# Two recurrent layers of a four-layer kernel: the state copies on ScalarE, and the group norm's power in two halves

## The chip, the cores and the metric

The kernel runs on one core of a Trainium2 chip. The core has a matrix engine (TensorE, PE in the profile; its weight loads are PEld), a vector engine (VectorE, DVE), an engine for activations (ScalarE, ACT), a programmable engine (GpSimd, POOL) and an engine that here only issues transfers (SyncE, SP). Each engine works through its own queue in order, and they meet through semaphores. The metric is the device time of one execution in microseconds (us), given as the median of several runs.

## The reference

Four layers run one after another on x of shape (4, 512, 512): an attention layer with 32 query heads and 8 key heads, two recurrent layers, and a last attention layer with an MLP of four times the width. The change touches the two recurrent layers alone. What they compute, for one batch, is this:

```python
k, v, w, r, g = ...                      # products of five mixes of x with its shifted self
w = exp(-exp(w))                         # per step and channel, in 32 heads of 16
def step(s, inp):                        # s: 16 x 16 state per head
    a = k_l[..., :, None] * v_l[..., None, :]
    out = einsum('bhs,bhst->bht', r_l, faaaa * a + s)
    return a + w_l[..., None] * s, out
y = scan over 512 steps of step
y = (y - mean(y)) * rsqrt(var(y) + 1e-5) # over the 16 channels of a head
x = x + (y * gn_w + gn_b) * silu(g) @ Wo.T
x = x + sigmoid(xr @ fWr.T) * (square(relu(xk @ fWk.T)) @ fWv.T)
```

The state starts from rows of the context `ctx_2048`, and everything is float32.

## The kernel before

The function `recurrent` cuts the two layers into 16 units (q = 0 to 15): layer, batch, and one of two halves of 256 time steps. An even q is a first half; an odd q continues it from the state that the even one left. A unit is computed by three generators, `mixes` (layer norm, mixes and the products k, v, r, g, w), `outputs` (group norm and Wo) and `channels` (the second part of the layer). In between runs the recurrence itself, in G = 8 groups per unit, with a running number g = 8q + (0 to 7).

The recurrence takes two time steps at once. For a group, `begun` multiplies on VectorE the spread-out v (vr, in PSUM) by k into two tiles, kv for the second and A for the first step of each pair (line 833), copies the start state S into column 0 of kv (line 839, VectorE), and adds A to kv with an accumulating transfer that GpSimd issues (`added`, line 584). ScalarE spreads the decay into W (line 844). `scan` then runs the scan over kv (line 862, VectorE), in even units copies the last column back into S (line 864, VectorE), and multiplies by r into two tiles ry (line 867, VectorE). `summed` sums ry over the channels on TensorE (py, line 881), and `taken` adds py to y (line 894, VectorE). The tile A has one buffer, kv two, and vr one.

The order of the work is written out by hand. The loop over g runs from before 0 to 28 beyond the last group (g = 128 = `end`); in every turn it calls `summed(g - 1)`, `begun(g + 1)`, `scan(g)`, and every fourth time `repeated` (vr, line 814), and then the pieces that are due in this turn, in four phases EARLY, SOON, MID and LATE. A generator's `yield 11, EARLY` says that its next piece belongs to turn 8q + 11, phase EARLY; `follow` appends it to the list `steps[(turn, phase)]`. So `outputs(q)` starts at turn 9 of its unit, while the unit q + 1 is in its group 1, and `channels(q)` at turn 19. What is called first stands first in each engine's queue. From turn 129 on, one piece of layer 3 (`beside`) is called after each turn's pieces.

The group norm of `outputs` is spread over these turns: the mean (turn 9), y minus the mean (line 909), the squares on ScalarE (line 912), the variance on TensorE (line 917), variance plus 1e-5 into `rstd`, a tile gn_rs of 128 x 64 (line 927, VectorE, turn 10 LATE), the power -1/2 on GpSimd (line 929, turn 11 EARLY), four copies into rp on ScalarE (line 933, turn 12 LATE), a product that spreads it over the channels (pbc, line 935; bc on ScalarE, line 938), and y times it (line 940). Then follow yg on ScalarE (line 945) and its product with the gate on GpSimd (line 952), and Wo.

In GpSimd's queue, the power of unit q - 1 stands in turn 8q + 3. Behind it stand, as `channels` and `mixes` of other units fall due: the small power of the next layer norm (rs_cx, line 79) with ln_mv (line 552), in the layers' later units the two transfers x<-xr (line 584), then the kv<-A of the next turn, mix_g<-xa, and the kv<-A of the turn after it. ScalarE's queue in an even unit has, in its groups 0 to 7 and among much else: al (line 792), mix (line 665), td (line 735), o_w (lines 744 and 750, twice exponential), o_v (line 702), bc (line 938), yg (line 945), and xk and xr (line 990). The gate is o_g: ScalarE writes its tanh (line 698) after GpSimd's yg has left that tile, and VectorE's line 717 finishes it, which frees a PSUM tile for TensorE's transposes ptn (line 572).

Of the kernel before, what the change touches and what calls it, by code (L numbers as in the profile page):

```python
# [11 lines left out]
ALU = mybir.AluOpType  # L12
# [18 lines left out]
def tile_xattn_rwkv_perceiver(ctx: ExitStack, tc: tile.TileContext, t: dict, out: bass.AP):  # L31
    nc = tc.nc
# [7 lines left out]
    mhalf = const.tile([P, TS // 4], F32, name="mhalf")  # L40
# [30 lines left out]
    def mm(ps, pairs):  # L71
        for i, (lhsT, rhs) in enumerate(pairs):
            nc.tensor.matmul(ps, lhsT, rhs, start=(i == 0), stop=(i == len(pairs) - 1))  # L73
# [22 lines left out]
    def psum_tile(shape, name):  # L96
        pool, tag = psum["p"]
        return pool.tile(shape, F32, tag=tag, name=name)
# [356 lines left out]
    def recurrent(lp, ep, beside):  # L455
# [5 lines left out]
        TP = TS // 2  # L461
        EARLY, SOON, MID, LATE = range(4)
# [67 lines left out]
        def flat(a):  # L530
            return a.rearrange("p a l -> p (a l)")
# [314 lines left out]
        def place(g):  # L846
            q, j = divmod(g, G)
            return q, j // NI, j % NI

        def quarters(kv):  # L850
            return kv.rearrange("p (q f) l -> p q f l", f=2)

        def states(q):
            return st[q]["S"].rearrange("p i (q e f) -> p i e q f", e=2, f=2)

        def scan(g):

            q, e, i = place(g)
            d = st[q]
            kv = kvs.pop(g)  # L860

            nc.vector.tensor_tensor_scan(flat(kv), flat(W[g % 2]), flat(kv), 0.0, ALU.mult, ALU.add)  # L862
            if units[q][2] == 0:
                nc.vector.tensor_copy(states(q)[:, i, e], quarters(kv)[:, :, :, TP])
            for h in range(2):
                y = ys[g, h] = mp.tile([P, 4, 2, TP], F32, tag="ry", name="ry", bufs=4)
                nc.vector.tensor_tensor(  # L867
                    y,
                    kv[:, 4 * h : 4 * h + 4, None, :TP].to_broadcast([P, 4, 2, TP]),
                    d["r"][:, i].rearrange("p (o m) -> p o m", o=2)[:, None].to_broadcast([P, 4, 2, TP]),  # L870
                    ALU.mult,
                )
# [23 lines left out]
        def outputs(q):  # L896

            li, b, hf = units[q]
            n = f"L{li}_"
            c, d = small[li], st[q]  # L900
            y = d["y"]
            NQ = TS // 4
            full = [P, NI, TS]
            pm = psum_tile([P, TS], "pmean")
            mm(pm, [(gmean, y[:, i, :]) for i in range(NI)])
            mean = sq.tile([P, TS], F32, tag="mean", name="mean", bufs=1)
            nc.scalar.copy(mean, pm)
            yield 9, LATE
            nc.vector.tensor_tensor(y, y, mean[:, None, :].to_broadcast(full), ALU.subtract)
            yield 10, EARLY  # L910
            y2 = mq.tile(full, F32, tag="cx", name="y2", bufs=BUFS["cx"])
            nc.scalar.activation(y2, y, AF.Square)
            yield 10, SOON
            var = psum_tile([P, NQ], "var")
            for i in range(NI):
                for a in range(4):
                    nc.tensor.matmul(
                        var[32 * a : 32 * a + 32],
                        gm32,
                        y2[:, i, NQ * a : NQ * a + NQ],  # L920
                        start=(i == 0),
                        stop=(i == NI - 1),
                        tile_position=(0, 32 * a),
                    )
            yield 10, LATE
            rstd = sq.tile([P, NQ], F32, tag="gn_rs", name="gn_rs")
            nc.vector.tensor_scalar(rstd, var, 1.0, 1e-5, ALU.mult, ALU.add)  # L927
            yield 11, EARLY
            nc.gpsimd.tensor_tensor(rstd, rstd, mhalf[:, :NQ], ALU.pow)  # L929
            yield 12, LATE  # L930
            for a in range(4):
                rs = slice(32 * a, 32 * a + 32)
                nc.scalar.copy(rp[rs, NQ * a : NQ * a + NQ], rstd[rs])
            yield 13, EARLY
            pm = psum_tile([P, TS], "pbc")
            mm(pm, [(gself, rp)])
            bc = sq.tile([P, TS], F32, tag="mean", name="bc", bufs=1)
            nc.scalar.copy(bc, pm)
            yield 13, LATE
            nc.vector.tensor_tensor(y, y, bc[:, None, :].to_broadcast(full), ALU.mult)  # L940
            yield 14, EARLY

            yg = mq.tile(full, F32, tag="cx", name="yg", bufs=BUFS["cx"])
            for i in range(NI):
                nc.scalar.activation(
                    yg[:, i].rearrange("p (m o) -> p o m", o=2),
                    y[:, i].rearrange("p (o m) -> p o m", o=2),
                    AF.Identity,
                    bias=c["gn"][:, i, 1:2],
                    scale=c["gn"][:, i, 0:1],  # L950
                )
            nc.gpsimd.tensor_tensor(yg, yg, d["g"], ALU.mult)
            yield 15, MID
            wo = wpool.tile([P, NI, C], F32, tag="w", name=n + "wo")
            for a in range(4):
                nc.sync.dma_start(
                    wo[32 * a : 32 * a + 32], t[n + "Wo"].rearrange("(h a i) n -> a h i n", a=4, i=NI)[a]
                )
            pms = []
            for lt in range(NT):  # L960
                pm = psum_tile([P, C], "pm")
                mm(pm, [(yg[:, i, lt * P : (lt + 1) * P], wo[:, i, :]) for i in range(NI)])
                pms.append(pm)
            yield 15, LATE
            for lt in range(NT):
                x = xn[b][hf * NT + lt]
                nc.vector.tensor_tensor(x, pms[lt], x, ALU.add)
# [74 lines left out]
        steps = {}  # L1042
# [6 lines left out]
        for q in range(len(units)):  # L1049
            if q > 0:  # L1050
                follow(q, (-13 if q == 1 else -11, LATE), mixes(q))
            follow(q, (9, EARLY), outputs(q))
            follow(q, (19, LATE), channels(q))
# [3 lines left out]
        with ExitStack() as below, ExitStack() as above:  # L1057
# [14 lines left out]
            for g in range(at[0], end + 28):  # L1072
                if 0 < g <= end:
                    summed(g - 1)
                if -1 <= g < end - 1:
                    begun(g + 1)
                if 0 <= g < end:
                    scan(g)
                if 0 < g < end - 2 and g % NI == NI - 2:
                    repeated(*place(g + 2)[:2])  # L1080
                for ph in (EARLY, SOON, MID, LATE):
                    for q, gen in steps.pop((g, ph), ()):
                        at = next(gen, None)
                        if at:
                            follow(q, at, gen)
                    if ph == MID and 0 < g <= end and g % NI == 0:
                        taken(g - 1)
                if g == end:
                    above.close()
                elif g > end:  # L1090
                    next(beside, None)
# [336 lines left out]
    with tc.manual_schedule(engines={E.PE, E.DVE, E.Activation, E.Pool}), ExitStack() as both:  # L1428
        lp = both.enter_context(tc.tile_pool(name="rl", bufs=1))
        ep = both.enter_context(tc.tile_pool(name="rt", bufs=2))  # L1430
        third = layer3()
        ahead = recurrent(lp, ep, iter(third.__next__, "closed"))
        layer0(ahead, ep)
        for _ in ahead:
            pass
        both.close()
        for _ in third:
            pass
# [64 lines left out]
```

## Time and profile before

| What | us |
|---|---|
| median of 3 runs | 3747.28 (3745.63 to 3757.73) |
| the profiled execution | 3749.93 |
| its span | 3748.2 |
| granted clock of TensorE, mean | 0.971 |
| first scan to last scan (line 862) | 782.8 to 2282.2 |

The span runs from the first instruction to the last; 1.7 us of the execution lie around it. Layer 0 fills about the first 780 us, the recurrent layers run to about 2440 us, their last part beside the start of layer 3, which then runs alone to the end. A unit of the recurrent layers takes some 98 us.

A row of the profile names the line, the engine, the operation and the tiles written and read; "x16" is how often it ran, and after the bar stand its busy time in all, the mean of one in ns, and the idle time of its engine just before it with what ended that. In a timeline a row has the start, the length, the engine and the instruction, and in brackets the idle time before it with what ended it. These are the rows of the page that belong to the recurrence:

| row | count | mean ns |
|---|---|---|
| line 862, VectorE, scan | 128 | 2316 |
| line 867, VectorE, ry | 256 | 1416 |
| line 833, VectorE, A | 128 | 1217 |
| line 584, GpSimd, issue of kv<-A | 127 | 936 |
| line 881, TensorE, py | 1024 | 631 |

The copies of line 864 took 172 to 2302 ns, median 174, 64 of them.

### The profile page before, as it was taken

The page shows a single profiled execution, that of the slowest core. Times are in us where ns is not written, and L with a number is a line of the kernel's source. Part 1 is how long each engine was busy: PE and PEld are TensorE (multiplying, and loading weights), DVE is VectorE, ACT ScalarE, POOL GpSimd, SP SyncE. Part 2 cuts the span into 40 slices and gives each one's busy share as a digit, 9 for nine tenths or more (in the row PEclk, how much of TensorE's full clock was granted, in tenths as well). Part 3 has the DMA queues.
Part 4 walks back from the last instruction along what each step waited for, and adds up shares of the span by engine and source line. Part 5 has one row for each costly group of instructions (what it writes and reads, how often), then busy time and mean ns, then how long its engine had stood idle before and what let it go on. Part 6 is the DMA issues. An engine that isn't in the chain of part 4 may idle for free.

```text
span 3748.2 us, 52355 instructions
## 1 busy us (share of the span) xinstructions
PE 3561.1 (95%) x20544; PEld 1894.1 (51%) x20544; DVE 2748.8 (73%) x4665; ACT 1667.2 (44%) x2486; POOL 1762.1 (47%) x834
## 2 busy tenths in 40 slices
PE   9999999998899999999999996999999999999989
PEld 3333333365565656656556653544455444544446
DVE  6777777679988888888988884388856666667531
ACT  4776776533444444444444432233344334334421
POOL 4777777524444444444444444155533433444430
PEclk9999998999899999999999998999999999999999
DMA  4000000056577777777777775410022112121223
GB/s 153 24 12 23 12 9 20 24 142 136 136 174 177 167 178 180 171 167 175 177 169 176 168 183 125 118 35 15 26 82 79 60 56 96 60 71 35 96 96 123
DMA packets 188805, 386.66 MB, mean 103 GB/s; under 512 B 18128, under 2 KB 44880, under 8 KB 186512
## 3 DMA queue, kind: packets, MB, share of 16 engines
q1 hardware_dynamic: 150256, 251.72, 21.3%
q0 software_dynamic: 38304, 131.61, 19.0%
q8 instruction: 162, 2.65, 0.3%
q14 instruction: 83, 0.68, 0.1%
HBM read 247.50 MB, written 4.19 MB: 67 GB/s over the span
## 4 chain that ended last, share of the span: by engine, by line
PE 72%; DVE 12%; DMA 5%; issue 4%; POOL 3%; ACT 3%; SPq 0%; POOLq 0%; DVEq 0%; ACTq 0%
PE pm L73 10%; PE ph L73 6%; PE pv L73 6%; PE po L73 6%; DMA kv<-A 5%; PE psc L242 5%; PE pst L279 5%; PE pst L1186 4%; PE psc L1186 4%; PE po L1252 3%; PE po L304 3%; PE pr L73 3%; PE pk L73 3%; DVE ry L867 3%; DVE kv L862 2%
## 5 line engine op out<-in xcount | busy, mean ns | idle before, releaser
L1247 POOL TENSOR_TENSOR acc<-acc,aT 128x2048 f32<-128x2048 f32 x96 | 436.2, 4544 | 337.9 <-ACT aT L1242 219.9
L292 POOL TENSOR_TENSOR aT<-aT,nmT 128x1536 f32<-128x1536 f32 x124 | 428.6, 3460 | 207.6 <-ACT aT L290 184.3
L254 DVE CUSTOM_DVE_ANT_0 sc<-psc,nm 128x512 f32<-128x512 f32 x512 | 354.1, 692 | 147.0 <-PE psc L242 89.3
L1231 DVE TENSOR_TENSOR aT<-pst,mb 128x512 f32<-128x512 f32 x512 | 317.8, 683 | 162.7 <-PE pst L1186 162.7
L867 DVE TENSOR_TENSOR ry<-kv,o_r 128x1024 f32<-128x1024 f32 x256 | 352.0, 1416 | 3.5
L862 DVE TENSOR_TENSOR_SCAN kv<-W,kv 128x1032 f32<-128x1032 f32 x128 | 296.4, 2316 | 0.2 <-DMA kv<-A 0.2
L584 POOL DMA_DIRECT2D kv<-A x127 | 118.9, 936 | 367.6 <-DVE kv L839 364.5
L290 ACT COPY aT<-pst 128x512 f32<-128x512 f32 x372 | 196.6, 595 | 178.0 <-PE pst L279 177.5
L298 ACT ACTIVATE aT<-aT 128x2048 f32<-128x2048 f32 x128 | 246.7, 1929 | 5.3 <-POOL aT L292 4.6
L73 PE MATMUL ph<-nT,l_m 128*128 128x256 f32 x1024 | 238.1, 388 | 0.0
L73 PE MATMUL po<-l_m,hT 128*128 128x512 f32 x512 | 233.1, 601 | 0.0
L73 PEld LDWEIGHTS ph<-nT,l_m 128*128 128x128 f32 x1024 | 193.4, 193 | 64.4 <-issue 24.8
L1200 DVE CUSTOM_DVE_ANT_0 sc<-psc,zeros,mx 128x512 f32<-128x512 f32 x256 | 176.7, 747 | 57.8 <-PE psc L1186 48.7
L279 PE MATMUL pst<-q,km 32*128 32x512 f32 x1024 | 206.4, 641 | 9.5 <-DVE mxs L254 5.8
L833 DVE TENSOR_TENSOR A<-vr,o_k 128x1024 f32<-128x1024 f32 x128 | 155.8, 1217 | 73.5 <-DMA kv<-A 73.5
L1242 ACT ACTIVATE aT<-aT 128x2048 f32<-128x2048 f32 x64 | 122.3, 1911 | 191.6 <-DVE aT L1231 191.4
L1240 ACT ACTIVATE aT<-aT,mc 128x2048 f32<-128x2048 f32 x64 | 128.1, 2002 | 162.3 <-DVE aT L1231 156.1
L1200 DVE CUSTOM_DVE_ANT_0 sc<-psc,nm 128x512 f32<-128x512 f32 x256 | 161.1, 686 | 52.2 <-PE psc L1186 52.2
L242 PE MATMUL psc<-km,q 32*128 32x512 f32 x1024 | 198.6, 650 | 0.8 <-ACT q L223 0.8
L881 PE MATMUL py<-ry,k 128*32 128x512 f32 x1024 | 161.1, 631 | 39.3 <-DVE ry L867 26.4
L929 POOL TENSOR_TENSOR gn_rs<-gn_rs,mhalf 128x64 f32<-128x64 f32 x16 | 186.4, 11648 | 24.7 <-DVE gn_rs L927 24.7
L1186 PE MATMUL psc<-kT,q 32*128 32x512 f32 x1024 | 171.0, 646 | 12.3 <-DVE aT L1231 11.5
(265 smaller groups left out, 7012.9 us busy)
## 6 DMA issues: line engine op xcount, KB each, us to landing
l_m<-in_L_W SPq DMA_DIRECT2D x64, 1024.0 KB, 5.1
kv<-A POOLq DMA_DIRECT2D x127, 516.0 KB, 7.4
L_wk<-in_L_Wk SPq DMA_DIRECT2D x16, 1024.0 KB, 8.0
L_wr<-in_L_Wr SPq DMA_DIRECT2D x16, 1024.0 KB, 7.5
L_wv<-in_L_Wv SPq DMA_DIRECT2D x16, 1024.0 KB, 6.0
L_wg<-in_L_Wg SPq DMA_DIRECT2D x16, 1024.0 KB, 7.8
L_wo<-in_L_Wo SPq DMA_DIRECT2D x64, 256.0 KB, 7.5
L_fk<-in_L_fWk SPq DMA_DIRECT2D x16, 1024.0 KB, 8.7
```

What stands on the lines that cost most here:

```text
L73: nc.tensor.matmul(ps, lhsT, rhs, start=(i == 0), stop=(i == len(pairs) - 1))
L242: nc.tensor.matmul(psc, d["q"][g][rs, lt * P : (lt + 1) * P], d["km"][rs, a, :], start=True, stop=True, tile_position=(32 * r, 0),)
L254: nc.vector.tensor_tensor_reduce(sc, ps[r], d["nm"][lt], 1.0, -3.0e38, ALU.add, ALU.max, mxs[:, a, lt, c : c + 1])
L279: nc.tensor.matmul(pst, d["km"][rs, a, s * P : (s + 1) * P], d["q2", a][rs, :], start=True, stop=True, tile_position=(32 * r, 0),)
L292: nc.gpsimd.tensor_tensor(w[:, n:, :], w[:, n:, :], nmT[:, None, :].to_broadcast([P, NR - n, L]), ALU.add)
L298: nc.scalar.activation(w, w, AF.Exp)
L862: nc.vector.tensor_tensor_scan(flat(kv), flat(W[g % 2]), flat(kv), 0.0, ALU.mult, ALU.add)
L867: nc.vector.tensor_tensor(y, kv[:, 4 * h : 4 * h + 4, None, :TP].to_broadcast([P, 4, 2, TP]), d["r"][:, i].rearrange("p (o m) -> p o m", o ...
L1186: nc.tensor.matmul(psc, lhsT[rs], rhs[rs], start=True, stop=True, tile_position=(32 * r, 0))
L1200: nc.vector.tensor_tensor_reduce(sc, ps[r], d["nm"][a], 1.0, mx[:, 0, lt, r : r + 1] if a else 3.0e38, ALU.add, ALU.min, mx[:, a, lt, r : ...
L1231: nc.vector.tensor_tensor(w[:, r, :], ps[r], d["mb"][:, r, :], ALU.subtract)
L1247: nc.gpsimd.tensor_tensor(d["acc", m], d["acc", m], w, ALU.add)
```

## The change

Two edits. In `scan`, the copy of the last column of kv into S, in even units, is no longer called on VectorE. A small generator `kept`, which holds the same copy as a ScalarE instruction, is put into the list for this turn's phase SOON. It is put there before the EARLY pieces of the turn are run, so it is the first of the SOON pieces, and stands in ScalarE's queue behind the EARLY pieces of the turn and ahead of its later ones. In `outputs`, the power is called on the left 32 columns of `rstd` in turn 11 EARLY and on the right 32 in turn 12 EARLY; the copies into rp stay in turn 12 LATE. Lines after the first edit are 4 later, after the second 6 later.

```diff
+        def kept(dst, src):
+            nc.scalar.copy(dst, src)
+            yield from ()
+
         def scan(g):
...
             nc.vector.tensor_tensor_scan(flat(kv), flat(W[g % 2]), flat(kv), 0.0, ALU.mult, ALU.add)
             if units[q][2] == 0:
-                nc.vector.tensor_copy(states(q)[:, i, e], quarters(kv)[:, :, :, TP])
+                steps.setdefault((g, SOON), []).append((q, kept(states(q)[:, i, e], quarters(kv)[:, :, :, TP])))
...
             nc.vector.tensor_scalar(rstd, var, 1.0, 1e-5, ALU.mult, ALU.add)
             yield 11, EARLY
-            nc.gpsimd.tensor_tensor(rstd, rstd, mhalf[:, :NQ], ALU.pow)
+            nc.gpsimd.tensor_tensor(rstd[:, : NQ // 2], rstd[:, : NQ // 2], mhalf[:, : NQ // 2], ALU.pow)
+            yield 12, EARLY
+            nc.gpsimd.tensor_tensor(rstd[:, NQ // 2 :], rstd[:, NQ // 2 :], mhalf[:, : NQ // 2], ALU.pow)
             yield 12, LATE
```

## Prediction, made before the changed kernel ran

> **What bounds the kernel now.** I read the page's busy shares first, then the stage of the recurrent layers (785 to 2290 us after the span's start), then who waits for whom there.
>
> ```profile
> PE 3561.1 (95%) x20544; PEld 1894.1 (51%) x20544; DVE 2748.8 (73%) x4665; ACT 1667.2 (44%) x2486; POOL 1762.1 (47%) x834
> L929 POOL TENSOR_TENSOR gn_rs<-gn_rs,mhalf 128x64 f32<-128x64 f32 x16 | 186.4, 11648 | 24.7 <-DVE gn_rs L927 24.7
> ```
>
> Two of these units, 98 us each, by windows (length, then busy time of TensorE, its weight loads, VectorE, ScalarE, GpSimd, then granted clock, DMA share, GB/s):
>
> ```profile
> 1766.00:1962.00 196.00, 185.81 (x1249) 118.31 (x1248) 171.70 (x176) 88.41 (x176) 90.58 (x61) 0.97 0.75 171
> ```
>
> TensorE is the bound: of two units (196 us) it works 185.8, VectorE 171.7. A unit's fixed small waits of TensorE add to 2.3 us (0.58, 0.49, 0.51 and 0.74, seen in every unit of its timeline), and neither edit touches what ends them. What a faster VectorE or GpSimd can give is in these rows, for 980 to 2280 us; the columns are total, times, longest:
>
> ```profile
> PE ptn L572 <- DVE o_g L717: 17.4, 11, 2.9
> PE vr L814 <- DVE A L833: 13.2, 7, 3.7
> ```
>
> and in VectorE's own row:
>
> ```profile
> DVE A L833 <- DMA kv<-A: 66.1, 36, 6.3
> ```
>
> So at most 30.6 us of TensorE's idle time hangs on a late VectorE, and VectorE itself waits 66.1 us for the accumulating transfer kv<-A, because A has one buffer. The order of time in one even unit shows why (first GpSimd, then VectorE, ScalarE, TensorE):
>
> ```profile
> 1762.43 0.85 POOL L584 DMA_DIRECT2D kv<-A  x1 [1.04 <-DVE kv L839]
> 1762.99 11.72 POOL L929 TENSOR_TENSOR gn_rs<-gn_rs,mhalf 128x64 f32<-128x64 f32 x1
> 1774.69 0.69 POOL L79 TENSOR_TENSOR rs_cx<-rs_cx,mhalf 128x2 f32<-128x2 f32 x1
> 1775.46 1.57 POOL L552 TENSOR_TENSOR ln_mv<-ln_mv,rs_cx 128x2 f32<-128x2 f32 x1
> 1776.98 1.81 POOL L584 DMA_DIRECT2D x<-xr  x2
> 1778.14 1.53 POOL L584 DMA_DIRECT2D kv<-A  x1
> ...
> 1769.80 1.22 DVE L833 TENSOR_TENSOR kv<-vr,o_k 128x1024 f32<-128x1024 f32 x1
> 1773.49 1.23 DVE L833 TENSOR_TENSOR A<-vr,o_k 128x1024 f32<-128x1024 f32 x1 [2.47 <-DMA kv<-A]
> ...
> 1787.89 1.23 DVE L833 TENSOR_TENSOR A<-vr,o_k 128x1024 f32<-128x1024 f32 x1 [2.50 <-DMA kv<-A]
> ...
> 1772.51 1.06 ACT L750 ACTIVATE o_w<-o_w 128x1024 f32<-128x1024 f32 x1
> ...
> 1813.40 1.11 PE L572 MATMUL ptn<-ident,z 128*128 128x128 f32 x4 [2.83 <-DVE o_g L717]
> ```
>
> The second kv<-A was ready at 1774.8 (end of the copy L839) and went out at 1778.1, after the power. Its landing, 9.7 us later, held A for 2.50 us; VectorE carried that lag to o_g, and TensorE stood 2.83 us before the row at 1813.40.
>
> **The power in two halves.** Removed: one 11.72 us row per unit. Added: two of 128x32. No such row exists; the same operation on 128x2 took 0.69 and on 128x64 11.72, so 128x32 is 0.69 + 30 x 0.178 = 6.0 us. Below, half of 11.72 (5.9); above, the whole 11.7 again, if the time belonged to the instruction; 0.69 speaks against that. I take 6.0.
>
> In GpSimd's queue the first half stays where the whole one was; then come rs_cx, ln_mv, the two x<-xr and the second kv<-A, and only then the second half, followed by mix_g and the third kv<-A. In odd units the first half ends 5.7 us sooner, rs_cx then waits only for VectorE's L78 (1868.9 in the unit at 1862), and kv<-A leaves as soon as its L839 is done, 3.3 to 6.1 us earlier than now. The second half ends about 1782.7 in the unit shown: before mix_g is ready (1784.3), and well before ScalarE's rp, which TensorE's product v holds until 1789.75. So it hides there.
>
> In VectorE's timeline, the wait at the A behind that transfer, which this can take away, is in units 1 to 15 2.3, 3.6, 2.9, 6.3, 5.4, 1.5, 3.1, 2.3, 0, 2.5, 2.1, 0.5, 5.8, 0.5 and 4.7 us. [...]
>
> **The state copies.** 64 leave VectorE. A row is 0.17 us, but the next instruction starts 0.08 after it: 64 x 0.08 = 5 us of VectorE. Those of 2.0 to 2.3 us stood behind a GpSimd product; ry stands there instead (in odd units, without a copy, it does so), so that is no gain. On ScalarE the nearest row is lastc, 0.20 us: 13 us of an engine that is busy 44%.
>
> What it adds is a wait: kv has two buffers, so VectorE's L833 of two groups on now waits until ScalarE has copied. Placing each copy in ScalarE's order of the changed program and its scan in the trace, 51 of 64 end at least 0.7 us before that. Group 1 of an even unit is 0.6 late in six units, which the next small waits of VectorE take up (0.24 us before gn_rs, and the copies no longer there). Group 3 is bad in the six even units from 1180 us on: its copy is queued behind o_w, which ends at 1773.57 by TensorE's pace, so L833 of 1769.80 starts at 1773.7, 3.9 late. A after it waited 2.47 anyway; net 1.4 us there, and 1.2, 0.8, 2.9, 3.3 and 3.4 in the others. Hence kv<-A leaves only 1.5 to 3.7 us sooner in even units, and their share of the waits above is 3.7, 1.5, 2.0, 2.0, 0.5, 0.5. The late ry must be there for py (TensorE, 1781.23): it ends at 1780.9, just in time. Group 7's copy can hold xr behind it for 1.1 to 3.0 us; xr's product starts 5 to 18 us after its landing now. SP's load of S now follows ScalarE's copies of a unit long past.
>
> **What TensorE makes of it.** For ptn the floor is 0.58 us, which the unit at 1715 shows with o_g in time: 17.4 - 11 x 0.6 = 10.8. Of the vr waits 13.2, I keep 2 (one of 3.02 follows a smaller gain). That is 22; the lags of the even units cost 2: **20**. Before 980 us one more ptn wait goes: **1.4**.
>
> Idle stretches also cost clock. Rows of the 3.4 us behind such a gap:
>
> ```profile
> 1215.60:1219.00 3.40, 3.40 (x15) 0.52 0.66 152
> 1813.40:1816.80 3.40, 3.40 (x8) 0.58 0.04 13
> ```
>
> Eight of ten such stretches ran at 0.50 to 0.71, two at 1.00. [...] The rows show it after 2.1 to 2.9 us too, and even after 0.5 us gaps (pr took 8.83 instead of 7.13 at 1652), so: eight x 3.4 x 0.45 = 12 us, of which half comes back elsewhere. I take **6**.
>
> **The ends.** The last scans (2242 to 2293) are VectorE's: A waits 4.67 us for a kv<-A that the power delayed; all up to the next fk product moves by **4.7**. In the very last unit it turns round. There the second half is queued behind rs_cx, which waits for VectorE's statistics, themselves behind TensorE's pv:
>
> ```profile
> 2314.88 10.57 POOL L929 TENSOR_TENSOR gn_rs<-gn_rs,mhalf 128x64 f32<-128x64 f32 x1 [24.75 <-DVE gn_rs L927]
> 2325.43 0.69 POOL L79 TENSOR_TENSOR rs_cx<-rs_cx,mhalf 128x2 f32<-128x2 f32 x1
> ...
> 2329.15 0.59 PE L73 MATMUL pbc<-rp,gsel 128*128 128x256 f32 x2
> ```
>
> rs_cx starts at 2324.3, the second half at 2326.5, ends 2332; rp, four copies of 0.25, ends at 2333.0; pbc waits until then: **-3.9**, and 1.5 for a cold clock.
>
> Sum: 20 + 1.4 + 6 + 4.7 - 3.9 - 1.5 = 26.7. The span 3748.2 becomes 3721.5; with 1.7 around it 3723.2 against the profiled run's 3749.93. That run lay 2.65 over the median 3747.28, so **3721 us**. 0.3% is 11 us, about what a measurement can tell.
>
> **Rivals.** (1) Absorbed, 3742 us. TensorE's ptn wait ends with ScalarE's o_g, which waits for GpSimd's yg (1809.9), and that follows TensorE's own xc. If VectorE's lead meets GpSimd's products again (each block 2 us), only the vr waits of units 4, 5 and 13 and the tail remain: 5 to 6. For it: 22.5 us of VectorE's own wait for o_g. Against: with VectorE in time, the unit at 1715 has 0.58.
>
> (2) Slower, 3763 us: the copies hold VectorE. The margin of ry before py is 0.4 us. If o_w's end plus the copy comes later than I put it, each even unit hands its whole 3.9 to TensorE: 6 x (3.5 + 1.5 clock) = 30, and the even units' half of the 26 is gone: -27 + 13 + 30 = +16. It decides from 2.3 us per even unit. Against: y L894 idles 4.9 us for py in the unit at 2175, so later groups catch up.
>
> (3) A half costs as much as the whole: kv<-A is as late as now, the third one 1.4 us later in 12 units, the last unit loses 9.5: 3773 us; it needs over 8 us a half.
>
> **Chances.** Forecast 0.72 (its own range 3704 to 3734: from 30.6 + 12 + 6.1 - 5.4 gained to half of the sum); absorbed 0.14; copies 0.11; (3) 0.03. Faster 0.72, within 0.3% 0.14, slower 0.14. The range 3703 to 3744 takes in the absorbed case and leaves out the slower ones and a little below.
>
> **What would show it.** Halves near 6.0 us; kv<-A in the step of the second half within 1 us of L839 in odd units; A waiting under 35 instead of 66 us; ptn <- o_g under 9 us in all; L833 in even units waiting for S on ScalarE, some 20 us in all, with py <- ry no longer than before; pbc in the last unit 4 us late. Wrong, if py waits over 2 us per even unit, or ptn keeps its 2.8.

## The result, and the profile after

The changed kernel took 3720.59 us (median of 4 runs, 3717.76 to 3726.57) beside 3748.63 us for the kernel before on the same chip: a ratio of 0.9915, 95% interval 0.9899 to 0.9931, so 28 us faster. The profiled run had 3717.76 us and a span of 3715.9, 32.3 less than before.

The groups of the two halves, from the view by lines (count, then busy time in all, mean ns, idle time before it):

```profile
L935 POOL TENSOR_TENSOR gn_rs<-gn_rs,mhalf 128x32 f32<-128x32 f32 x16 | 103.7, 6482 | 0.0
L933 POOL TENSOR_TENSOR gn_rs<-gn_rs,mhalf 128x32 f32<-128x32 f32 x16 | 102.8, 6426 | 18.7 <-DVE gn_rs L931 18.7
```

A half takes 6.4 to 6.5 us; the two together cost 1.3 us a unit more than the whole 11.65. The second is never held up (0.0).

Who waits for whom, in 976 to 2247 us (the same work as 980 to 2280 before; total, times, longest):

```profile
PE ptn L572 <- DVE o_g L717: 9.3, 12, 2.9
PE vr L814 <- DVE A L833: 3.0, 2, 2.5
...
DVE A L833 <- DMA kv<-A: 11.2, 10, 2.6
DVE kv L833 <- ACT S L857: 25.1, 12, 3.9
PE py L885 <- DVE ry L871: 18.2, 16, 4.0
```

VectorE's wait for kv<-A fell from 66.1 to 11.2 us, TensorE's two waits behind it from 17.4 and 13.2 to 9.3 and 3.0. The row of L857 is new: the wait that the state copies brought. TensorE's wait for ry (the last row), which it might have lengthened, is 18.2 us; in the kernel before it was 18.9.

The timeline of the unit shown before (GpSimd, then VectorE and ScalarE):

```profile
1739.34 0.85 POOL L584 DMA_DIRECT2D kv<-A  x1 [0.95 <-issue]
1739.90 6.37 POOL L933 TENSOR_TENSOR gn_rs<-gn_rs,mhalf 128x32 f32<-128x32 f32 x1
1746.57 0.70 POOL L79 TENSOR_TENSOR rs_cx<-rs_cx,mhalf 128x2 f32<-128x2 f32 x1 [0.30 <-DVE rs_cx L78]
1747.35 0.20 POOL L552 TENSOR_TENSOR ln_mv<-ln_mv,rs_cx 128x2 f32<-128x2 f32 x1
1747.57 1.82 POOL L584 DMA_DIRECT2D x<-xr  x2
1753.16 0.86 POOL L584 DMA_DIRECT2D kv<-A  x1 [3.78 <-ACT o_k L702]
1753.72 6.37 POOL L935 TENSOR_TENSOR gn_rs<-gn_rs,mhalf 128x32 f32<-128x32 f32 x1
...
1749.98 0.19 ACT L857 COPY S<-kv 128x8 f32<-128x8 f32 x1
1750.19 1.22 DVE L833 TENSOR_TENSOR kv<-vr,o_k 128x1024 f32<-128x1024 f32 x1 [3.70 <-ACT S L857]
...
1760.67 1.21 DVE L833 TENSOR_TENSOR kv<-vr,o_k 128x1024 f32<-128x1024 f32 x1
1761.80 1.21 DVE L833 TENSOR_TENSOR A<-vr,o_k 128x1024 f32<-128x1024 f32 x1
```

VectorE stands 3.70 us for ScalarE's copy, and the second kv<-A still goes out 0.53 us after its L839 instead of 3.34 us. It lands 4.8 us later (9.7 before), and the next A starts with no wait. The second half ends at 1760.1 and rp is written at 1766.2, so the half hides.

What other transfers are under way at that time differs too. SyncE's loads of weights, first before, then after:

```profile
1779.41 3.90 SPq L956 DMA_DIRECT2D L_wo<-in_L_Wo  x4
```

```profile
1755.90 1.79 SPq L962 DMA_DIRECT2D L_wo<-in_L_Wo  x4
```

Before, the second kv<-A went out 0.5 us behind the later x<-xr and 1.3 us ahead of the first of these loads; now it stands 5.0 us behind the one and 2.7 us ahead of the other.

The same two units by windows (length, busy time of TensorE, its weight loads, VectorE, ScalarE, GpSimd, granted clock, DMA share, GB/s):

```profile
1640.00:1836.00 196.00, 188.42 (x1295) 119.13 (x1296) 171.20 (x176) 89.22 (x184) 91.08 (x66) 1.00 0.78 180
```

TensorE gets through 1295 rows in the time that held 1249, at a clock of 1.00 instead of 0.97.

Between the first and the last product vr TensorE's account can be closed. Before, then after:

```profile
775.60:2232.90 1457.30, 1359.94 (x9344) 863.08 (x9340) 1279.52 (x1334) 640.78 (x1269) 655.28 (x430) 0.97 0.73 168
```

```profile
773.40:2200.00 1426.60, 1343.14 (x9345) 855.50 (x9341) 1260.49 (x1270) 649.53 (x1333) 636.38 (x444) 0.98 0.75 172
```

The stretch is 30.7 us shorter. Idle time (length less busy) fell from 97.4 to 83.5 us, 13.9 less. The other 16.8 us are TensorE's busy time, for the same products: they ran at a better clock, 0.98 instead of 0.97 in the mean. Cut into windows of 3.4 us, the stretch before has 16 groups of windows below full clock, the one after 7; what goes before a group is shown in the last experiment.

### The profile page after: what moved, and what is told of

Its sections match the earlier page's. It is cut to its first block, busy times and chain, and to the rows that moved or that the text cites. A ratio compares the mean times of both kernels' runs of the same rounds, so it can differ in the third digit from the quotient of the medians.

```text
span 3715.9 us, 52436 instructions
## 1 busy us (share of the span) xinstructions
PE 3545.8 (95%) x20544; PEld 1885.9 (51%) x20544; DVE 2728.7 (73%) x4601; ACT 1675.7 (45%) x2550; POOL 1743.4 (47%) x850
## 5 line engine op out<-in xcount | busy, mean ns | idle before, releaser
L871 DVE TENSOR_TENSOR ry<-kv,o_r 128x1024 f32<-128x1024 f32 x256 | 398.6, 1598 | 7.2 <-PE pm L73 0.5
L584 POOL DMA_DIRECT2D kv<-A x127 | 111.4, 877 | 358.0 <-DVE kv L839 220.0
L1192 PE MATMUL pst<-q,kT 32*128 32x512 f32 x1024 | 183.1, 649 | 0.0
L1192 PE MATMUL psc<-kT,q 32*128 32x512 f32 x1024 | 171.0, 644 | 12.3 <-DVE aT L1237 11.5
L1251 POOL TENSOR_TENSOR acc<-aT 128x2048 f32<-128x2048 f32 x16 | 72.5, 4532 | 234.2 <-ACT aT L1246 234.2
```

The costliest lines, as they stand in the source:

```text
L871: nc.vector.tensor_tensor(y, kv[:, 4 * h : 4 * h + 4, None, :TP].to_broadcast([P, 4, 2, TP]), d["r"][:, i].rearrange("p (o m) -> p o m", o ...
L1192: nc.tensor.matmul(psc, lhsT[rs], rhs[rs], start=True, stop=True, tile_position=(32 * r, 0))
```

## Experiments

The runs were made on three chips, on which the kernel before took 3748.60, 3750.25 and 3753.42 us. A ratio is to the kernel before on the same chip; a difference of a few us between two runs of different chips means little.

### One edit alone

The first two runs make one edit of the two: in the first the power stays as in the kernel before, in the second the copies do.

```diff
             yield 11, EARLY
-            nc.gpsimd.tensor_tensor(rstd[:, : NQ // 2], rstd[:, : NQ // 2], mhalf[:, : NQ // 2], ALU.pow)
-            yield 12, EARLY
-            nc.gpsimd.tensor_tensor(rstd[:, NQ // 2 :], rstd[:, NQ // 2 :], mhalf[:, : NQ // 2], ALU.pow)
+            nc.gpsimd.tensor_tensor(rstd, rstd, mhalf[:, :NQ], ALU.pow)
```

> State copies on ScalarE, the power whole and where it was. My theory (the gain comes from the second kv<-A no longer standing behind the power): close to before, 3742 to 3753 us; VectorE's A still waits some 50 to 66 us for kv<-A, and kv waits for S on top. Rival (the copies that left VectorE made the gain): 3718 to 3730 us, and A's wait falls under 30 us.

Measured: 3738.34 us beside 3748.60, ratio 0.9971 (0.9957 to 0.9985). Neither expectation was met: the copies alone gain 10 us, and A still waits 47.4 us for kv<-A.

```diff
             if units[q][2] == 0:
-                steps.setdefault((g, SOON), []).append((q, kept(states(q)[:, i, e], quarters(kv)[:, :, :, TP])))
+                nc.vector.tensor_copy(states(q)[:, i, e], quarters(kv)[:, :, :, TP])
```

> The power in two halves in turns 11 and 12, the copies still on VectorE. My theory: all of the change's gain or a little more, 3714 to 3723 us; A waits 8 to 16 us for kv<-A, no wait of kv for S, so the kv<-A of an even unit's group 5 leaves about 4 us earlier than in the changed kernel. Rival (both edits are needed): 3730 to 3742 us.

Measured: 3721.07 us, ratio 0.9916 (0.9897 to 0.9935). The halves alone bring all of the gain, and the copies nothing on top of them. A waited longer than the 8 to 16 us that I expected, 23.6 us, though kv did not wait for S; the two waits of VectorE together were 36.3 us in the changed kernel (11.2 and 25.1). The second kv<-A of the even units from 4 on left 0.9 to 3.7 us sooner behind the first than in the changed kernel, not some 4. The lag of VectorE that the copies bring did not reach TensorE.

Why do the copies gain when they are alone? The unit at 1766 in the run with copies alone (VectorE, then GpSimd):

```profile
1765.97 1.23 DVE L833 TENSOR_TENSOR kv<-vr,o_k 128x1024 f32<-128x1024 f32 x1 [3.87 <-ACT S L857]
1767.11 1.21 DVE L833 TENSOR_TENSOR A<-vr,o_k 128x1024 f32<-128x1024 f32 x1
...
1768.31 2.30 DVE L866 TENSOR_TENSOR_SCAN kv<-W,kv 128x1032 f32<-128x1032 f32 x1
...
1777.57 1.21 DVE L833 TENSOR_TENSOR A<-vr,o_k 128x1024 f32<-128x1024 f32 x1
...
1755.51 11.48 POOL L933 TENSOR_TENSOR gn_rs<-gn_rs,mhalf 128x64 f32<-128x64 f32 x1
...
1767.74 0.19 POOL L552 TENSOR_TENSOR ln_mv<-ln_mv,rs_cx 128x2 f32<-128x2 f32 x1
...
1769.13 1.54 POOL L584 DMA_DIRECT2D kv<-A  x1
```

The stall of 3.87 us puts kv behind o_w, so the state copy into kv that lets kv<-A go ends 1.4 us after the power instead of 0.1; GpSimd's small ln_mv runs ahead of VectorE's scan, and kv<-A leaves 0.7 us after its L839, not 3.3. The wait at the A behind it, 2.50 us before, is gone. That shows where the gain can come from. To test it, I left on VectorE only the copies whose wait stands behind o_w, those of group 3 (power whole, all other copies on ScalarE):

```diff
+            if units[q][2] == 0 and g % G == 3:
+                nc.vector.tensor_copy(states(q)[:, i, e], quarters(kv)[:, :, :, TP])
-            if units[q][2] == 0:
+            elif units[q][2] == 0:
                 steps.setdefault((g, SOON), []).append((q, kept(states(q)[:, i, e], quarters(kv)[:, :, :, TP])))
```

> Copies on ScalarE, the power whole and in its place, but the copy of group 3 of each even unit stays on VectorE, so that kv of group 5 does not wait for ScalarE behind o_w. Theory (the copies alone gained because this stall shifts A of group 5 behind o_w and GpSimd's small ln_mv ahead of VectorE's scan): the gain goes, 3744 to 3752 us, and A of group 6 waits 0.5 to 6 us again in even units. Rival (they gained because VectorE has 64 instructions less): 3736 to 3741 us as with all copies moved.

Measured: 3753.32 us beside 3750.25, ratio 1.0006 (0.9994 to 1.0017), 1.3 us above the range of the theory. With 56 of 64 copies still moved the gain is gone. So it was not the work taken from VectorE that gained; what is left is the shift by the stall. A waits 63.7 us for kv<-A again (66.1 before, 47.4 with all copies moved). At group 6 it waited in units 4, 6, 10 and 14 (1.2 to 5.9 us); in 8 and 12 it did not, against the theory. That the two edits do not add up fits: both take away the same waits of even units.

### Splitting or moving?

Two kernels with the copies on ScalarE: both halves back to back in turn 11, and the power whole in turn 12.

```diff
             yield 11, EARLY
             nc.gpsimd.tensor_tensor(rstd[:, : NQ // 2], rstd[:, : NQ // 2], mhalf[:, : NQ // 2], ALU.pow)
-            yield 12, EARLY
             nc.gpsimd.tensor_tensor(rstd[:, NQ // 2 :], rstd[:, NQ // 2 :], mhalf[:, : NQ // 2], ALU.pow)
+            yield 12, EARLY
```

> Copies on ScalarE, both halves back to back in turn 11, so that kv<-A stands behind both. My theory (the place in GpSimd's queue counts, not that the instruction is shorter): no better than the copies alone, 3742 to 3755 us. [...]

Measured: 3744.76 us, ratio 0.9977 (0.9966 to 0.9989), no better than the copies alone. Here splitting gave nothing without the kv<-A in between.

```diff
             yield 11, EARLY
-            nc.gpsimd.tensor_tensor(rstd[:, : NQ // 2], rstd[:, : NQ // 2], mhalf[:, : NQ // 2], ALU.pow)
             yield 12, EARLY
-            nc.gpsimd.tensor_tensor(rstd[:, NQ // 2 :], rstd[:, NQ // 2 :], mhalf[:, : NQ // 2], ALU.pow)
+            nc.gpsimd.tensor_tensor(rstd, rstd, mhalf[:, :NQ], ALU.pow)
```

> Copies on ScalarE, the power whole but in turn 12, behind the second kv<-A. My theory: the second kv<-A is in time, but the 11.7 us then hold back the third one by 1 to 4 us and end after 1788 of the before timeline, near where rp is needed: 3722 to 3737 us, and in the last unit pbc some 9 to 10 us late. Rival (a long power hurts wherever it stands): 3742 us or more. Second rival (any place behind the second kv<-A is as good as the split): within 2 us of the changed kernel.

Measured: 3760.79 us, ratio 1.0025 (1.0014 to 1.0036): slower than before, and my 3722 to 3737 was wrong by over 20 us. The timeline of an even unit:

```profile
1769.21 11.48 POOL L934 TENSOR_TENSOR gn_rs<-gn_rs,mhalf 128x64 f32<-128x64 f32 x1
...
1780.65 0.88 POOL L584 DMA_DIRECT2D mix_g<-xa  x1
1781.25 1.18 POOL L584 DMA_DIRECT2D kv<-A  x1
...
1793.37 1.22 DVE L833 TENSOR_TENSOR A<-vr,o_k 128x1024 f32<-128x1024 f32 x1 [5.51 <-DMA kv<-A]
1794.65 2.09 PE L814 MATMUL vr<-o_v,vsel 32*128 32x512 f32 x8 [2.71 <-DVE A L833]
```

The power now holds the third kv<-A (its L839 is done at 1778.6) for 2.7 us, and that one takes 12 us to land. It goes out at the same moment as a load of weights:

```profile
1781.24 0.39 SPq L63 DMA_DIRECT2D L_fk<-in_L_fWk  x1
```

So it does in the six even units from unit 4 on, where it lands in 10.4 to 12.1 us; in the changed kernel the load follows 2.1 us behind the third kv<-A of these units, which lands in 5.6 to 6.7. In the unit shown A waits 5.51 us and TensorE 2.71. I had priced the delay of the issue and not the longer landing. In the unit shown of the changed kernel the kv<-A go out at 1739.3, 1753.2 and 1763.6: gaps of 13.8 us, of which rs_cx, ln_mv, x<-xr and the issue itself take 4, and of 10.4. The whole power fits in neither, 6.4 us in both. In the last unit pbc stood 9.54 us, as expected; in units 0, 1 and 14 it stood 4.2 to 6.4 us as well, which I had not put.

### The last unit

The power stays whole in the last unit alone, once with the change and once without its copies.

```diff
+            if q == len(units) - 1:
+                nc.gpsimd.tensor_tensor(rstd, rstd, mhalf[:, :NQ], ALU.pow)
+            else:
+                ...
```

> The changed kernel, but in the last unit the power stays whole and in turn 11. My theory (in the last unit the second half stands behind the small power rs_cx and holds rp, pbc and everything up to the end): 3715 to 3718 us, 3 to 6 us under the changed kernel; pbc no longer waits 4.4 us there. Rival (the end is set by other waits, on fk and on layer 3's pieces): within 2 us of the changed kernel, 3719 to 3722 us.

> The halves alone, copies on VectorE, and in the last unit the power whole. By my theory for the last unit 3715 to 3718 us, since the copies on ScalarE add nothing to the halves; if the last unit's rp does not set the end, 3720 to 3722 us.

Measured: 3713.69 us (3709.98 to 3719.41; before 3750.25), ratio 0.9903 (0.9886 to 0.9919), and 3716.35 us, 0.9909 (0.9894 to 0.9924). The first is just under its range, the second in it. Each is below its pair with the split last unit, by 6.9 and 4.7 us in the times and, as the chips differ, by 4.5 and 2.6 us in the ratios. The intervals of the ratios overlap, so the times alone do not settle it; the trace does for the wait. The last unit of the changed kernel shows where they come from:

```profile
2283.49 1.83 POOL L584 DMA_DIRECT2D x<-xr  x2
2284.69 6.11 POOL L935 TENSOR_TENSOR gn_rs<-gn_rs,mhalf 128x32 f32<-128x32 f32 x1
2290.83 1.00 ACT L939 COPY rp<-gn_rs 32x64 f32<-32x64 f32 x4 [6.07 <-POOL gn_rs L935]
...
2291.89 1.22 PE L73 MATMUL pbc<-rp,gsel 128*128 128x256 f32 x2 [4.41 <-ACT rp L939]
```

and the first of the two kernels:

```profile
2274.71 10.57 POOL L934 TENSOR_TENSOR gn_rs<-gn_rs,mhalf 128x64 f32<-128x64 f32 x1 [24.12 <-DVE gn_rs L931]
...
2288.98 0.59 PE L73 MATMUL pbc<-rp,gsel 128*128 128x256 f32 x2
```

The wait of 4.41 us is gone. This version, the change with the last unit's power whole, had the lowest median of all kernels here.

### What an idle stretch of TensorE costs

Over half of the gain between the first and last vr was clock. To price it, ScalarE writes the squares y2 several times over in the changed kernel, which makes TensorE's idle stretch before var longer, once in each unit; nothing else is added. The diff is that of the run with three squares; the others have two and five.

```diff
-            nc.scalar.activation(y2, y, AF.Square)
+            for _ in range(3):
+                nc.scalar.activation(y2, y, AF.Square)
```

> The changed kernel with ScalarE's squares y2 written three times over, which makes TensorE wait some 1.9 us longer for var, once in each of 16 units. If an idle stretch of about 2.4 us costs clock as I put it (3.4 us at 0.55): TensorE's idle time grows by 25 to 32 us and its busy time by another 15 to 25 us, together 3760 to 3778 us. If only idle stretches of 3.4 us and more cost clock: busy time as in the changed kernel within 4 us, together 3745 to 3754 us. If the wait is absorbed: under 3735 us.

> The changed kernel with the squares y2 written twice, so that TensorE's stretch before var is about 1.6 us instead of 0.5. From the run with three (gap 2.69 us, idle time 24 us and busy time 23 us over the changed kernel): if the price in clock goes with the length of the gap, idle grows by 12 us and busy by 8 to 12 us, 3740 to 3745 us. If there is a threshold between 0.7 and 2.7 us and 1.6 is under it: busy within 4 us of the changed kernel, 3730 to 3736 us. If any gap over some 0.7 us costs the same: busy by 20 us or more, 3750 us and over.

> The changed kernel with the squares y2 written five times over, TensorE's stretch before var about 4.8 us. If the price in clock goes with the length of the gap: busy time 40 us and more over the changed kernel. If it is one slow stretch for each gap, however long: idle grows by some 50 us, busy by 20 to 28 us as with gaps of 2.69 us, together 3792 to 3802 us.

Times in us, and idle and busy time between the first and last vr, worked out as above:

| squares written | idle stretch before var | time | idle | busy |
|---|---|---|---|---|
| 1 (the change) | 0.51 | 3720.59 | 83.5 | 1343.1 |
| 2 | 1.60 | 3744.80 | 92.1 | 1355.5 |
| 3 | 2.69 | 3772.91 | 107.7 | 1366.5 |
| 5 | 4.86 | 3814.37 | 134.1 | 1374.2 |

With three squares the time and the busy time came in the ranges put (23.4 us of busy time more) and the idle time just under (24.2). With two, the time fell where a price in proportion would have it; with five it lay outside both forecasts. So no price by length alone holds, and the windows show why. The slow stretches of a trace do not start at any time: their starts lie whole multiples of 3.413 us apart, to 0.01 us over the whole span in the kernel before (34 stretches) and in the changed one (25), and to 0.1 us between the first and the last vr of the eight other traces that were cut into windows of 3.4 us. Cut at these times, the windows around one stretch of 2.69 us (three squares) are these (length, TensorE's busy time, granted clock, DMA share, GB/s):

```profile
1765.04:1768.45 3.41, 1.29 (x34) 1.00 0.98 305
1768.45:1771.86 3.41, 3.41 (x5) 0.50 1.10 229
1771.86:1775.28 3.42, 3.42 (x9) 1.00 1.07 213
```

The window in which TensorE works 1.29 of 3.41 us is followed by one at half the clock, which loses 3.41 x 0.5 = 1.7 us of work. One slow window followed the stretch in each of the twelve units between 1070 and 2170 us. Around one stretch of 1.60 us (two squares) and one of 4.86 us (five):

```profile
1748.89:1752.30 3.41, 1.90 (x35) 1.00 0.89 260
1752.30:1755.71 3.41, 3.41 (x9) 1.00 1.10 253
```

```profile
1784.93:1788.34 3.41, 0.00 (x0) 1.00 0.89 264
1788.34:1791.75 3.41, 2.09 (x34) 0.50 1.07 246
1791.75:1795.17 3.42, 3.42 (x6) 0.50 0.67 133
```

A stretch of 1.60 us leaves more than half of any window, and none of the twelve cost clock. One of 4.86 us cost two slow windows in each of the twelve; of the two shown 1.3 us lay still in the stretch, so 2.8 us of work were lost. That the place on these windows counts, and not the length, two waits of the kernel before show, the first of 2.90 us (1517.96 to 1520.86), the second of 2.93 (1615.99 to 1618.92):

```profile
1515.85:1519.26 3.41, 2.11 (x28) 1.00 0.48 126
1519.26:1522.68 3.42, 1.82 (x7) 1.00 0.51 198
1522.68:1526.09 3.41, 3.41 (x9) 1.00 0.21 39
1614.83:1618.25 3.42, 1.16 (x12) 1.00 0.64 232
1618.25:1621.66 3.41, 2.74 (x7) 0.50 0.20 75
```

The first is split between two windows, each busy for over half, and costs nothing; the second falls for the most part into one. In the traces of the kernel before and of the changed one, between 780 and 2250 us, each of the 17 windows at full clock in which TensorE worked for less than 0.46 of the length was followed by a slow one; of those with 0.48 and more ten were, all with products pmm in them (0.53 to 0.85). With three squares the units lie some 99.2 us apart, 29.1 windows, so the twelve stretches fell on nearly the same place, each with 1.88 us or more in one window: that 2.69 us always costs is not shown.

What remains is pmm. With two squares, two windows there were these:

```profile
1728.41:1731.82 3.41, 2.82 (x19) 1.00 0.41 132
1731.82:1735.23 3.41, 3.41 (x13) 0.50 1.08 299
```

TensorE stands only 0.59 us in the first, between its products pmm, and the next is slow, in six of the twelve units, every other one. There two units take 194.56 us, 57.0 windows, and one about half of that, so the same stop falls on two places in turn. These six slow windows, and not the longer stretches, are most of the 12.4 us of busy time that this run has more. In the changed kernel two units between 1030 and 2200 us went slow behind such stops. Why a slow window follows one with 2.82 us of work there is open.

## Why the prediction was right, point by point

**The time and the mechanism.** 3721 was forecast and 3720.59 measured. The cause was as put: the second kv<-A no longer stands behind the power. The run with both halves together rules out the shorter instruction by itself, the run with the halves alone rules out that the copies are needed.

**A half** was put at 6.0 us and took 6.4 to 6.5. It hides behind rp in all units but the last, where pbc stood 4.41 us, and unit 14, where it stood 1.3. The rival that a half costs as much as the whole fell with the first row.

**kv<-A** was to leave within 1 us of L839 in odd units: 0.3 us in seven of the eight, 1.25 in unit 13. A's wait was put under 35 us and was 11.2: too careful. I had left the even units a lag; their waits of 0.5 to 6.3 us at group 6 are gone from unit 4 on, since the transfer, issued 2.8 us sooner after its L839, also lands sooner (4.8 instead of 9.7 us), clear of x<-xr and of the loads L_wo. That is the term I did not have, and its like at the third kv<-A is part of what made the power moved whole so bad.

**The copies.** VectorE's work falls by 5 us (1265.3 with the halves alone, 1260.5 with both), as put. L833 waits 25.1 us for S, put at some 20. Their price for TensorE was put at 2 us and the rival that they make the kernel slower at 3763; 3721.07 without and 3720.59 with them leave no price to be seen.

**TensorE's waits.** In the same stretch ptn went from 17.4 to 9.3 us and vr from 13.2 to 3.0: 18.3 us, where 20 were put (22 less 2 for the lags). Eleven of the twelve ptn waits are 0.55 to 0.60, the floor that was put at 0.6. The twelfth, of 2.9 us at 1023, stands in a unit where the kernel before had none, and the halves alone show it too; its cause is open. The 1.4 us before 980 did not come: that ptn wait was 1.36 and is 1.37, and a wait of vr there grew from 2.2 to 4.0. So all idle time between the first and the last vr fell by 13.9 us, where 21.4 were put (20 and 1.4): this term was too large.

**The clock** was too small, in the step "so: eight x 3.4 x 0.45 = 12 us, of which half comes back elsewhere. I take **6**." Busy time fell by 16.8 us, more than the whole 12; that half comes back elsewhere was an estimate, and no run shows it. The two misses nearly cancel: 27.4 put, 30.7 measured. To that extent it is luck that the forecast came within 1 us. The 12 us, priced by the rows behind such gaps, were nearer than half of them. In the traces of the kernel before and of the changed one each slow stretch of these layers ran at 0.50 for 3.41 us or a multiple of it; and with three squares one came behind a window that had 1.29 of 3.41 us of work in it.

**The power beside VectorE's products.** Nothing was counted for it. In the kernel before, all 33 products ry that lie wholly inside a power took 1.22 to 1.23 us each, while beside GpSimd's 128x1024 product ruk one took up to 3.40 (two took 4.29 us at 1901.12; beside the power two took 2.35 at 1764.46). In the timeline of the changed kernel the products beside a half are as long as ever, and all 60 ry that lie wholly inside a half took 1.22 to 1.27 us each:

```profile
1739.90 6.37 POOL L933 TENSOR_TENSOR gn_rs<-gn_rs,mhalf 128x32 f32<-128x32 f32 x1
1741.05 2.36 DVE L871 TENSOR_TENSOR ry<-kv,o_r 128x1024 f32<-128x1024 f32 x2
```

**The ends.** The last scans were put at 4.7 us, and 1.8 came by the end of the last py in the changed kernel (5.2, 5.3 and 4.0 in the three other runs with halves). The last unit was put at -3.9: pbc waited 4.41, and keeping the power whole there gave 2.6 to 6.9, by the run and by whether times or ratios are compared. For the clock behind that wait 1.5 was put: the 3.41 us from 2291.73 ran at 0.50 and held 3.25 us of TensorE's work, so 1.6 us were lost.

## What to carry to other kernels

On an engine that both computes and issues transfers, ask of each long instruction which issue stands behind it and whether it fits into the gap between two of them: splitting alone gave nothing, moving alone made the kernel slower, and a half in each gap gave 0.85%. In the last round of a pipeline the later place has nothing to hide behind (4.41 us of pbc's wait here), so leave the work whole there. Ask also what other transfers go out around the moment to which an issue is moved. And price a stall of TensorE at its length plus the clock that it costs, taken from windows cut where the slow stretches of the same trace start: here each of 17 windows of 3.41 us with less than 0.46 of work was followed by one at half the clock, 1.7 us where TensorE worked all through it, while a stall of 2.90 us split between two windows cost none.

## What the runs showed that was not expected

- The second kv<-A of units 3 to 14 landed 7.6 to 12.3 us after its issue in the kernel before, where it left 3.3 to 6.1 us late, and 4.8 to 6.3 us after it in the changed kernel. Lateness by itself is not the reason: in units 1 and 2 of the kernel before it left 5.0 and 6.4 us late, with no x<-xr ahead of it and no load of weights issued in the 2 us behind it, and landed in 4.9 and 4.7 us; in the changed kernel it left on time there, amid four loads L_wo, and took 7.1 and 7.7. With x<-xr 0.5 us ahead and no load (unit 15 before) it took 6.3 us; units 3 to 14 had x<-xr there and loads L_wo from 0.4 us ahead to 2.2 us behind. No run moves these transfers alone, so this is read from the traces and not tested.
- GpSimd's ln_mv on 128x2 took 1.57 us beside VectorE's scan (1775.46 to 1777.03 in the kernel before, the scan's end), and 0.19 to 0.20 us at the shortest, while ry did not lengthen beside the power. So the two engines seem to get in each other's way here, but not in that pair.
- TensorE's clock fell to half for 3.41 us behind a stop of 0.59 us between products pmm and stayed at 1.00 behind one of 1.60 us in the same unit.
